# Counts for half blocks spread between the steps of two gates, and two ScalarE tables loaded ahead

## The chip, the cores and the metric

The kernel runs on one core of a Trainium2 chip. A core has five engines, each with an instruction stream of its own that runs in order: TensorE (PE; its weight loads are listed as PEld), VectorE (DVE), ScalarE (ACT), GpSimd (POOL) and SyncE (SP). [...] Transfers run on 16 DMA engines and are issued from the queues of SP, ACT and POOL; an issuing engine stands still while an issue waits. The metric is the device time of one execution in microseconds (us), as the median of several runs, lower being better.

## The reference

The input `x` has 8 × 256 rows of 512. Two layers follow one another, each added to its input:

```python
x = x + _L0_xattn_ref(_layernorm(x), k, fside_S2_0, ctx_2048, ctx_2048, 8)
x = x + _L0_ffn_ref(_layernorm(x), gate_w, shared_wg, ..., exp_wd)
```

The first layer is a long convolution by FFT of products of `v` with the context, per head (32 heads), summed with the context again. The second is a mixture of experts:

```python
scores = sigmoid(xf @ gate_w.T)
topk_w, topk_idx = top_k(scores, 2)
topk_w = topk_w / (topk_w.sum(-1) + 1e-20) * 2.5
shared_out = silu(xf @ shared_wg.T) * (xf @ shared_wu.T) @ shared_wd.T
h = silu(einsum('td,efd->etf', xf, exp_wg)) * einsum('td,efd->etf', xf, exp_wu)
routed_out = (topk_w[..., None] * einsum('etf,edf->etd', h, exp_wd)[topk_idx, t]).sum(1)
```

There are 2048 tokens, 8 experts of width 352 and a shared expert of width 704; each token goes to its two best experts.

## The kernel before

The 2048 rows are 16 tiles of 128 rows, and the tokens of the second layer are 4 chunks of 4 tiles. The order of all instructions is written out by hand (`tc.manual_schedule()`): an engine executes its instructions in the order in which the Python code emits them. Three stages follow one another.

**The loop over 32 heads** (lines 1481 to 1639) computes the convolution with products of Toeplitz matrices on TensorE (`conv_products`), weighs and sums on VectorE (`weigh`), and puts steps of the shared expert of the chunks that are ready between them. For a step that is a "seven" (seven products of half blocks in place of eight, `begin_seven`), `between` starts the first two products amid the head's convolution, and `copies`, called when the convolution is emitted, has ScalarE copy their results out of PSUM.

**The stage between** (lines 1642 to 1806) has no convolution left. It finishes the last tile's normalisation, the routing of the last chunk, the counts from which the blocks of tokens follow, and the table of tokens. The generator `rest_of_steps` supplies TensorE with the remaining steps of the shared expert, and `advance(n)` lets it run n pieces on, so the code alternates by hand between the two. Within it, a step's front products and their copies are emitted first, then `settle()` does what the steps before owe on VectorE and ScalarE, then come the step's other products. What a step owes is held in the list `owed`:

- for a down step, `rest` (line 1031): two adds of L1033 and two stores from SP's queue;
- for a seven of the up step, `gate` (line 912): it asks for a load of later weights, adds on VectorE (L914), and applies SiLU on ScalarE (L916). It returns `up`, whose add (L920) and multiply (L923) `settle` emits behind all gates.

The steps at issue are the last chunk's, c = 3, of which ft counts the tiles of the shared expert's width. In ft = 0 to 4, `product(1, p21, 3, ...)` writes the bank that the copies of `back` read, so it waits for a copy of L861 that stands behind a SiLU of L916 in ScalarE's order.

The counts: `route_places` (L793 to L804) gives each token its place and has POOL scatter the table's entries (L806); `block_experts` (L1147 to L1200) counts full blocks; `half_experts` (L1203 to L1294) counts half blocks, some 45 small VectorE instructions that mostly depend on one another. Its results are `eh` (the experts of half blocks), `any_half` (a matrix that picks the table's rows, read by TensorE in `half_slots`) and `used` (how many half blocks there are). They are emitted in one piece ahead of `advance(9 + 7 + 3)`, so all of them stand before the gates' adds of ft 0 and 1 in VectorE's order. `load_table` (L1299, SP) then brings the table, and `slots` and `half_slots` turn it into row numbers and gates with products L1326 to L1348.

ScalarE holds one set of function tables at a time. A load (ACT_TABLE_LOAD) is placed by the compiler ahead of a function whose set isn't there. The root (L329), SiLU (L916) and the sigmoid (L728 and, where c is 2, L977) are of different sets; copies and scaling by Identity need none of their own. The last tile's chain through ScalarE is: SiLU of the last seven of chunk 2, root of the variance (L329), normalisation (L354), a copy (L441), then four transposes on TensorE (L359).

**The block stage** (lines 1811 to 2021) goes through 33 blocks of up to 128 token rows: POOL gathers rows (L1732), SP stores and brings them back in squares (L1741, L1748), VectorE transposes (L1782, L1890), TensorE multiplies (up L1836, down L1906), ScalarE scales (L1915), and POOL adds the result into the output by a scatter (L1919). The shared expert's last two tiles are computed last and added to rows that are loaded when the scatters have ended (L2007 to L2021).

Of the kernel before, what the change touches and what calls it, by code (L numbers as in the profile page):

```python
# [8 lines left out]
F32 = mybir.dt.float32  # L9
I32 = mybir.dt.int32  # L10
# [5 lines left out]
P = 128  # L16
# [66 lines left out]
def tile_xattn_moe(  # L83
# [77 lines left out]
    ones = const.tile([P, P], F32, name="ones")  # L161
    G.memset(ones, 1.0)

    A.activation(const.tile([P, 1], F32, name="table_first"), ones[:, :1], AF.Sqrt)
    filler = rows.tile([P, 2 * P], F32, tag="xg", name="filler")
    G.memset(filler, 0.0)
    ident = kept.tile([P, P], F32, name="ident")
# [725 lines left out]
    def begin_seven(c, ft):  # L893

        n = c * NSF + ft
        w = ups.pop(n)
        if not isinstance(w, list):
            w = [w[:, b] for b in range(14)]
        if ft == 0:
            hTs[c] = held.tile([P, NSF, TC], F32, tag="hT", name=f"hT_{c}")  # L900
        pair = ps_acc.tile([P, 2, TC], F32, tag="acc", name=f"gu_{c}_{ft}")
        g = shp.tile([P, TC], F32, tag="g", name=f"g_{c}_{ft}", bufs=2)
        u = hTs[c][:, ft, :]

        def rhs(k, at):
            return xfT[c][:, k : k + 2].rearrange("p k i t -> p k (i t)")[:, :, at]

        first, second = slice(0, HT), slice(HT, TC)
        moving = rhs(0, first), rhs(2, first), rhs(2, second), tbs[c]
        front, front_copies, back, free_of, products, copied = seven(pair, w, moving, g, u)  # L910

        def gate():
            ask(n)
            ins = V.tensor_tensor(pair[:, 0], pair[:, 0], g, ALU.add)  # L914
            free_of(ins, products[1] + copied[1][-1:])
            silu = A.activation(g, pair[:, 0], AF.Silu)  # L916

            def up(parts=(0, 1)):
                if 0 in parts:
                    ins = V.tensor_tensor(pair[:, 1], pair[:, 1], u, ALU.add)  # L920
                    free_of(ins, [silu])
                if 1 in parts:
                    V.tensor_tensor(u, pair[:, 1], g, ALU.mult)  # L923

            return up

        return front, front_copies, back, gate
# [4 lines left out]
    def seven_step(c, ft):  # L932
        at = up_step, c, ft
        if at not in begun:
            begun[at] = begin_seven(c, ft)
            yield from begun[at][0]()
            begun[at][1]()
        _, _, back, gate = begun.pop(at)
        yield from back()
        owed.append(gate)  # L940

    asks, held_back = [], [False]

# [199 lines left out]
    def g(name, s, dtype=F32):  # L1143
        return const.tile(s, dtype, name=name)
# [58 lines left out]
    def half_experts(kinds, both_kinds, ends):  # L1203

        nblk, halves, fours = [kinds[:, n] for n in range(3)]
        most = NEXP - 1
        V.tensor_scalar(nblk, nblk, 2.0, None, ALU.mult)
        first = g("first", [P, NEXP])
        V.tensor_tensor(first, nblk, first_of, ALU.add)
        bounds = g("bounds", [P, 2 * NEXP])  # L1210
        V.tensor_scalar(bounds[:, :NEXP], ends[:, 0], 2.0, None, ALU.mult)
        begin = g("begin", [P, 1])
        V.tensor_scalar_max(begin, bounds[:, most:NEXP], 2.0 * NDYN)
        V.tensor_scalar(bounds[:, NEXP:], ends[:, 1], begin, None, ALU.add)
        skip_by = g("skip_by", [P, 2 * NEXP])
        V.tensor_scalar(skip_by[:, :NEXP], nblk, -1.0, float(HALVES), ALU.mult, ALU.add)
        V.tensor_tensor(skip_by[:, NEXP:-1], skip_by[:, :most], nblk[:, 1:], ALU.add)
        V.tensor_tensor(skip_by[:, NEXP:-1], skip_by[:, NEXP:-1], halves[:, :most], ALU.subtract)
        turn = skip_by[:, most:NEXP]
        V.tensor_scalar(turn, turn, nblk[:, 0:1], bounds[:, most:NEXP], ALU.add, ALU.add)  # L1220
        V.tensor_scalar(turn, turn, begin, -float(HALVES * NEXP), ALU.subtract, ALU.add)
        V.memset(skip_by[:, -1:], -1e5)
        n = NHALF // 2
        segs = [P, n, 2 * NEXP]
        scratch = small.tile([P, TC], F32, tag="lg", name="past_half")
        past = scratch[:, : n * 2 * NEXP].rearrange("p (i e) -> p i e", e=2 * NEXP)
        half = g("half", [P, NHALF])
        for at in (slice(0, n), slice(n, NHALF)):
            V.tensor_tensor(
                past,  # L1230
                halfno[:, at].unsqueeze(2).to_broadcast(segs),
                bounds.unsqueeze(1).to_broadcast(segs),
                ALU.is_ge,
            )
            V.tensor_tensor(past, past, skip_by.unsqueeze(1).to_broadcast(segs), ALU.mult)
            V.tensor_reduce(half[:, at], past, AX.X, ALU.add)
        V.tensor_tensor(half, half, halfno, ALU.add)


        which = g("which", [P, NEXP])  # L1240
        V.scalar_tensor_tensor(which, fours, float(FOURS), ends[:, 2], ALU.mult, ALU.add)
        V.tensor_tensor(first, first, both_kinds, ALU.add)
        V.scalar_tensor_tensor(first, first, float(FOURS), fours, ALU.add, ALU.mult)
        behind = g("behind", [P, 1])
        V.tensor_scalar_max(behind, bounds[:, 2 * NEXP - 1 :], float(SURE_ENDS))
        more_fours = fourno[:, NFOUR:]
        V.tensor_scalar(more_fours, more_fours, behind, None, ALU.subtract)
        V.scalar_tensor_tensor(
            more_fours, more_fours, float(FOURS + 1 + NFOUR), more_fours, ALU.is_ge, ALU.mult
        )  # L1250
        any_four = [P, NFOUR + NCOND, NEXP]
        found = scratch[:, : (NFOUR + NCOND) * NEXP].rearrange("p (i e) -> p i e", e=NEXP)
        V.tensor_tensor(
            found,
            fourno.unsqueeze(2).to_broadcast(any_four),
            which.unsqueeze(1).to_broadcast(any_four),
            ALU.is_equal,
        )
        V.tensor_tensor(found, found, first.unsqueeze(1).to_broadcast(any_four), ALU.mult)
        four = g("four", [P, NFOUR + NCOND])  # L1260
        V.tensor_reduce(four, found, AX.X, ALU.add)
        tail = half[:, NPAIR:]
        V.scalar_tensor_tensor(tail, four, -float(FOURS), tail, ALU.add, ALU.max)

        experts = [P, NHALF, NEXP - 1]
        past = scratch[:, : NHALF * (NEXP - 1)].rearrange("p (i e) -> p i e", e=NEXP - 1)
        V.tensor_tensor(
            past,
            half.unsqueeze(2).to_broadcast(experts),
            expert_thresh.unsqueeze(1).to_broadcast(experts),  # L1270
            ALU.is_ge,
        )
        of = g("of", [P, NHALF])
        V.tensor_reduce(of, past, AX.X, ALU.add)
        eh = kept.tile([P, NHALF], I32, name="eh")
        V.tensor_copy(eh, of)

        V.scalar_tensor_tensor(of, of, -float(HALVES), half, ALU.mult, ALU.add)
        V.tensor_scalar(
            of, of, float(HALVES - FIXED_ENDS), -float(HALVES), ALU.is_ge, ALU.mult  # L1280
        )
        V.scalar_tensor_tensor(half, of, float(FIXED_ENDS), half, ALU.add, ALU.add)
        V.tensor_scalar(own_block, own_block, lane, None, ALU.is_equal)
        any_half = g("any_half", [P, 2, NHALF])
        for n in range(2):
            V.tensor_scalar(any_half[:, n], half, float(-n), lane2, ALU.add, ALU.is_equal)

        used = kept.tile([P, 1], I32, name="used")
        spare_fours = g("spare_fours", [P, 1])
        V.tensor_scalar(  # L1290
            spare_fours, ends[:, 2, most:], -float(NFOUR), 0.0, ALU.add, ALU.max
        )
        V.tensor_tensor(used, spare_fours, behind, ALU.add)
        return eh, any_half, used  # L1294

    def load_table():

# [183 lines left out]
    for h in range(H):  # L1481
# [21 lines left out]
        if ready and is_begun(*steps[done][1:]):  # L1503

            def between(at=steps[done][1:]):
                begun[at] = (begin_seven if at[0] is up_step else begin_down)(*at[1:])
                for _ in begun[at][0]():
                    pass

            def copies(at=steps[done][1:]):  # L1510
                begun[at][1]()

        held_back[0] = not odd and t - 1 in SQUARES
# [181 lines left out]
    route_T(last_c)  # L1695
    route_scores(last_c, lambda: advance(1))
    route_pick(last_c)
    advance(7)
    route_ranks(last_c)
    route_places(last_c)  # L1700
    ek, pick, *kinds = block_experts()
    eh, any_half, used = half_experts(*kinds)
    advance(9 + 7 + 3)
    tab = load_table()
    advance(4 + 6)
    load_wgu(4)
    advance(4)
    slots(tab, pick)
# [406 lines left out]
```

## Time and profile before

| | |
|---|---|
| median of 3 runs | 731.85 us (731.7, 731.85, 733.65) |
| the profiled execution's own time | 732.95 us |
| its span in the trace | 731.2 us |
| granted TensorE clock, mean | 0.998 |
| TensorE busy | 719.9 us |
| VectorE, ScalarE, POOL busy | 536.6, 227.5, 406.7 us |
| mean DMA rate | 181 GB/s |

A row of a timeline reads: start, duration, engine, line, operation, output and inputs, shape, number; in brackets, the idle time of the engine before it and what ended that. Times count from the start of the span. `PE` rows are products, modelled to their end, so that rows in sequence overlap a little. A line such as L916 is the line in the kernel's source before the change; behind the change the numbers are higher by 1 to 21.

### The profile page before, as it was taken

The numbers are of one execution on the slowest core, as the hardware profiler recorded it, in microseconds if no ns is written. First come the engines' busy times: TensorE is split into PE (matmuls) and PEld (weight loads), VectorE is DVE, ScalarE is ACT, GpSimd is POOL, SyncE is SP. The second block draws the span as 40 slices with busy tenths as digits, with TensorE's granted clock in tenths as the row PEclk, the third lists the DMA queues.
The fourth block names the chain that finished last, engine by engine and source line by source line (L and its number), as shares of the span: only waits on it lengthen the run. The fifth ranks groups of instructions, "written<-read, shape, count | busy, mean of one in ns | idle before, by whom it ended". The sixth has DMA issues, their size and how long they took to land.

```text
span 731.2 us, 10342 instructions
## 1 busy us (share of the span) xinstructions
PE 719.9 (98%) x3189; PEld 386.7 (53%) x3189; DVE 536.6 (73%) x1212; ACT 227.5 (31%) x459; POOL 406.7 (56%) x436
## 2 busy tenths in 40 slices
PE   9999999999999999999999999999999999999996
PEld 4333336555555655555665478455544553455552
DVE  4788889878777987777987584296767676767750
ACT  2222245745426554426435122111111111111110
POOL 7899998489876388784380422114244444453221
PEclk9999999999999999999999999999999999999999
DMA  8658748555624565623436968699975667567424
GB/s 301 239 178 284 278 146 278 170 121 189 227 89 158 180 158 151 226 94 122 151 69 191 384 169 278 185 268 287 284 174 112 126 140 189 126 134 170 82 34 86
DMA packets 91566, 132.16 MB, mean 181 GB/s; under 512 B 10928, under 2 KB 54960, under 8 KB 91504
## 3 DMA queue, kind: packets, MB, share of 16 engines
q1 hardware_dynamic: 69936, 93.89, 40.7%
q0 software_dynamic: 8544, 17.34, 13.1%
q10 hardware_dynamic: 13024, 20.19, 8.0%
q8 instruction: 28, 0.46, 0.3%
q14 instruction: 34, 0.28, 0.1%
HBM read 93.86 MB, written 37.52 MB: 180 GB/s over the span
## 4 chain that ended last, share of the span: by engine, by line
PE 62%; DMA 20%; issue 7%; DVE 5%; POOL 2%; ACT 2%; SPq 1%; POOLq 0%; DVEq 0%; ACTq 0%
PE cv L514 23%; PE gu L849 15%; DMA out_dram<-ys,row 11%; PE up L1836 7%; DMA out_dram<-ys,second_row 4%; PE dn L849 3%; PE y L1906 3%; PE same L556 2%; PE dn L1006 2%; PE gu L971 2%; DMA xv_d<-xn 2%; PE dn L1084 1%; POOL picked L1732 1%; DMA xq_f<-xn_d 1%; ACT xn L354 1%
## 5 line engine op out<-in xcount | busy, mean ns | idle before, releaser
L514 PE MATMUL cv<-kv,tz 64*64 64x512 f32 (+1 forms) x976 | 184.5, 597 | 0.0
L1836 PE MATMUL up<-wgu_sb,xT 128*128 128x352 f32 (+5 forms) x784 | 162.3, 460 | 0.4 <-PEq L1947 0.4
L1890 DVE STREAM_TRANSPOSE hTb<-h 32x96 f32<-32x96 f32 (+1 forms) x512 | 133.8, 261 | 7.8
L465 POOL TENSOR_TENSOR kv<-vT,ctxT 128x512 f32<-128x512 f32 x127 | 131.7, 1070 | 11.2 <-DVE top L748 3.9
L1836 PEld LDWEIGHTS up<-wgu_sb,xT 128*128 128x128 f32 (+2 forms) x784 | 92.5, 155 | 74.5 <-issue 37.2
L514 PEld LDWEIGHTS cv<-kv,tz 64*64 64x64 f32 (+1 forms) x976 | 65.1, 145 | 109.4 <-issue 88.0
L1919 POOL DMA_INDIRECT out_dram<-ys,row x33 | 50.5, 1530 | 119.0 <-ACT ys L1915 62.8
L1906 PE MATMUL y<-wd_sb,hTb 128*128 128x512 f32 (+11 forms) x294 | 90.7, 594 | 0.0
L590 DVE TENSOR_TENSOR prod<-cv,ctxT 128x1024 f32<-128x1024 f32 x64 | 78.2, 1221 | 16.1 <-PE cv L514 14.3
L849 PE MATMUL gu<-tb,wst 128*128 128x256 f32 x320 | 78.6, 381 | 1.3 <-ACT g L861 1.1
L599 DVE TENSOR_REDUCE convT<-prod 128x128 f32<-128x1024 f32 x64 | 78.1, 1220 | 2.2
L1732 POOL DMA_INDIRECT picked<-xn_d,row x33 | 35.3, 1068 | 67.0 <-DMA picked_d<-picked 26.5
L849 PEld LDWEIGHTS gu<-tb,wst 128*128 128x128 f32 x320 | 60.3, 190 | 18.1 <-issue 7.9
L1915 ACT ACTIVATE ys<-y,gate 128x512 f32<-128x512 f32 x33 | 22.7, 687 | 142.5 <-PE y L1906 138.0
L849 PE MATMUL gu<-xfT,wst 128*128 128x256 f32 x240 | 60.1, 386 | 1.0 <-DVE cv L587 1.0
L645 POOL TENSOR_TENSOR skip<-ctxT,w 128x512 f32<-128x512 f32 x16 | 17.3, 1078 | 73.8 <-ACT w L637 43.6
L1906 PEld LDWEIGHTS y<-wd_sb,hTb 128*128 128x128 f32 (+5 forms) x294 | 34.8, 155 | 42.7 <-issue 37.8
L1858 DVE TENSOR_TENSOR h<-h,up 128x352 f32<-128x352 f32 x32 | 16.7, 520 | 54.4 <-PE up L1836 52.1
L849 PEld LDWEIGHTS gu<-xfT,wst 128*128 128x128 f32 x240 | 44.2, 190 | 19.4 <-issue 11.3
L514 PE MATMUL cv<-kv,td 128*128 128x512 f32 x88 | 45.2, 596 | 0.0
L806 POOL DMA_INDIRECT table<-entries,to x32 | 31.6, 988 | 18.9 <-DVE to L804 8.1
L1851 ACT ACTIVATE h<-up 128x352 f32<-128x352 f32 x33 | 15.3, 464 | 73.5 <-PE up L1836 73.5
(269 smaller groups left out, 830.7 us busy)
## 6 DMA issues: line engine op xcount, KB each, us to landing
wst<-wst_d SPq DMA_DIRECT2D x17, 896.0 KB, 7.3
tz<-in_toep_dram SPq DMA_DIRECT2D x32, 384.0 KB, 3.2
wgu_sb<-in_egu_dram ACTq DMA_DIRECT2D x3, 2816.0 KB, 15.4
picked_d<-picked SPq DMA_DIRECT2D x33, 256.0 KB, 2.2
xg<-picked_d SPq DMA_DIRECT2D x132, 64.0 KB, 3.2
ctxT<-in_cT_dram SPq DMA_DIRECT2D x16, 384.0 KB, 4.8
x<-in_xv_dram SPq DMA_DIRECT2D x16, 256.0 KB, 3.7
x<-in_x_dram SPq DMA_DIRECT2D x16, 256.0 KB, 6.0
```

What stands on the lines that cost most here:

```text
L465: engine.tensor_tensor(kvs[h][:, at], v[:, :, cols].unsqueeze(2).to_broadcast([P, B, NH, NH]), ctxT[t][:, at, :, cols].unsqueeze(3).to_bro ...
L514: return T.matmul(banks[lb][cols], lhsT=w, rhs=x, start=first, stop=all(left[lb][n] == 0 for n in here),)
L590: V.tensor_tensor(prod, ps.rearrange("p k b j i -> p (k b) j i"), ctxT[t][:, 2 + 2 * n : 4 + 2 * n, :, cols] .rearrange("p k b i -> p (k b ...
L599: V.tensor_reduce(convT[t][:, two, :, cols].rearrange("p k b j -> p (k b) j"), prod, AX.X, ALU.add)
L806: ins = G.indirect_dma_start(out=table, out_offset=bass.IndirectOffsetOnAxis(ap=to[:, i : i + 1], axis=0), in_=entry[:, i, n, :], in_offse ...
L849: ins = T.matmul(ps, lhsT=w[2 * a + k], rhs=x[:, k], start=start and k == 0, stop=k == 1, skip_group_check=True,)
L1732: G.indirect_dma_start(out=picked[:n], out_offset=None, in_=xn_d, in_offset=bass.IndirectOffsetOnAxis(ap=row[:n, b : b + 1], axis=0), boun ...
L1836: ins = T.matmul(ps[at, m, :FF], lhsT=xTs[k][:, j].rearrange("p c b -> p (c b)")[:, at], rhs=weights(wgu_sb, k, e, (m * NLB + j) * FF, FF) ...
L1890: V.transpose(hT[q * Q : (q + 1) * Q, :n, c], hk[c * Q : (c + 1) * Q, q * NF * Q : (q * NF + n) * Q].rearrange("p (t a) -> p t a", a=Q),)
L1906: T.matmul(ps[at], lhsT=hT[:fw, ft].rearrange("p c b -> p (c b)")[:, at], rhs=weights(wd_sb, k, e, ft * L, L)[:fw], start=(ft == 0), stop= ...
L1915: A.activation(y[:n], ps[:n], AF.Copy, scale=gate[:n, k : k + 1])
L1919: ins = G.indirect_dma_start(out=out, out_offset=bass.IndirectOffsetOnAxis(ap=index[: at.stop - at.start, col : col + 1], axis=0), in_=y[a ...
```

## The change

`half_experts` becomes a generator. It emits everything up to L1248 at once and hands out its three result tiles, which are now allocated there; the rest is cut in five pieces. A new function `count_on` lets it go on by one piece. `gate` calls it behind the SiLU, and `up` behind the add and behind the multiply, so the pieces fall between the instructions of the gates of ft 0 and ft 1 of the last chunk. The list `counts_left`, which is empty at all other times, says whether there is anything to hand out; what is left after `advance(4 + 6)` is emitted then.

Besides, ScalarE applies SiLU to one column of a constant tile in two places: in head 31, ahead of the front copies of the last seven of chunk 2, and after `route_pick` of the last chunk. The compiler then places the loads of SiLU's table there.

```diff
-    A.activation(const.tile([P, 1], F32, name="table_first"), ones[:, :1], AF.Sqrt)
+    table_first = const.tile([P, 2], F32, name="table_first")
+    A.activation(table_first[:, 0:1], ones[:, :1], AF.Sqrt)
...
             silu = A.activation(g, pair[:, 0], AF.Silu)
+            count_on()
 
             def up(parts=(0, 1)):
                 if 0 in parts:
                     ins = V.tensor_tensor(pair[:, 1], pair[:, 1], u, ALU.add)
                     free_of(ins, [silu])
+                    count_on()
                 if 1 in parts:
                     V.tensor_tensor(u, pair[:, 1], g, ALU.mult)
+                    count_on()
...
+    counts_left = []
+
+    def count_on():
+        for rest in counts_left:
+            next(rest, None)
...
+        eh = kept.tile([P, NHALF], I32, name="eh")
+        any_half = g("any_half", [P, 2, NHALF])
+        used = kept.tile([P, 1], I32, name="used")
+        yield eh, any_half, used
         any_four = [P, NFOUR + NCOND, NEXP]
...
         V.tensor_tensor(found, found, first.unsqueeze(1).to_broadcast(any_four), ALU.mult)
+        yield
         four = g("four", [P, NFOUR + NCOND])
...
         V.scalar_tensor_tensor(tail, four, -float(FOURS), tail, ALU.add, ALU.max)
+        yield
...
         V.tensor_reduce(of, past, AX.X, ALU.add)
-        eh = kept.tile([P, NHALF], I32, name="eh")
+        yield
         V.tensor_copy(eh, of)
...
         V.scalar_tensor_tensor(half, of, float(FIXED_ENDS), half, ALU.add, ALU.add)
+        yield
         V.tensor_scalar(own_block, own_block, lane, None, ALU.is_equal)
...
         V.tensor_tensor(used, spare_fours, behind, ALU.add)
-        return eh, any_half, used
+        yield
...
             def copies(at=steps[done][1:]):
+                if h == H - 1:
+                    A.activation(table_first[:, 1:2], ones[:, 1:2], AF.Silu)
                 begun[at][1]()
...
     route_pick(last_c)
+    A.activation(table_first[:, 1:2], ones[:, 1:2], AF.Silu)
     advance(7)
     route_ranks(last_c)
     route_places(last_c)
     ek, pick, *kinds = block_experts()
-    eh, any_half, used = half_experts(*kinds)
+    counts_left.append(half_experts(*kinds))
+    eh, any_half, used = next(counts_left[0])
     advance(9 + 7 + 3)
     tab = load_table()
     advance(4 + 6)
+    for _ in counts_left.pop():
+        pass
     load_wgu(4)
```

## The prediction

> **What bounds the kernel now.** The page comes first: TensorE (PE) works through nearly the whole span, so only what lets it stand still, or what follows its last product, can change the time.
>
> ```profile
> span 731.2 us, 10342 instructions
> PE 719.9 (98%) x3189; PEld 386.7 (53%) x3189; DVE 536.6 (73%) x1212; ACT 227.5 (31%) x459; POOL 406.7 (56%) x436
> ```
>
> 11.3 us of the span are without a product. The timeline of TensorE, read for the rows that carry an idle time, says where: 1.32 at the start, 0.63 near 110 us, 0.96 at 388.99 (behind a VectorE add, L587), 0.45 at 571.87 (a branch), the last 6.5 or so behind the last product, and two places in the stretch that the change touches. Here they are with the group ahead of each:
>
> ```profile
> 400.69 1.02 PE L971 MATMUL gu<-xfT,wst 128*128 128x512 f32 x2
> 402.43 0.66 PE L359 MATMUL ptf<-ident,xn_kqa 128*128 128x128 f32 x4 [0.71 <-ACT xn_kqa L441]
> ...
> 432.27 1.89 PE L849 MATMUL gu<-xfT,wst 128*128 128x256 f32 x8
> 434.85 1.99 PE L849 MATMUL gu<-tb,wst 128*128 128x256 f32 x8 [0.69 <-ACT g L861]
> ```
>
> Groups overlap by some 0.16 us, so a bracket understates a stop. By starts: 10 products of L1006 take 4.29 in the chain, 0.43 each, so the transposes could begin at 400.69 + 0.86 = 401.55, and began 0.88 late; 8 rows of L849 take 1.73 (430.54 to 432.27), so the second group could begin at 434.00, and began 0.85 late.
>
> What held ScalarE there, by its timeline:
>
> ```profile
> 385.59 0.59 ACT L562 COPY same<-same 128x512 f32<-128x512 f32 x1
> 390.12 0.37 ACT L861 COPY g<-gu 128x256 f32<-128x256 f32 x1 [3.95 <-PE gu L849]
> ...
> 396.99 1.28 ACT L916 ACT_TABLE_LOAD   x1 [0.45 <-DMA xq_f<-xn_d]
> 398.28 0.60 ACT L916 ACTIVATE g<-gu 128x512 f32<-128x512 f32 x1
> 398.89 1.28 ACT L329 ACT_TABLE_LOAD   x1
> 400.19 0.29 ACT L329 ACTIVATE rstd_last<-mv_last,eps 128x1 f32<-128x1 f32 x1
> 400.91 0.81 ACT L354 ACTIVATE xn<-x,nb_last,rstd_last 128x512 f32<-128x512 f32 x1 [0.43 <-DVE nb_last L350]
> ...
> 408.25 0.18 ACT L728 ACTIVATE plT<-logit 128x32 f32<-128x32 f32 x1
> 424.70 0.37 ACT L861 COPY g<-gu 128x256 f32<-128x256 f32 x1 [16.26 <-PE gu L849]
> ...
> 431.60 0.37 ACT L861 COPY hT<-gu 128x256 f32<-128x256 f32 x1 [0.49 <-PE gu L849]
> 431.99 1.28 ACT L916 ACT_TABLE_LOAD   x1
> 433.93 0.60 ACT L916 ACTIVATE g<-gu 128x512 f32<-128x512 f32 x1 [0.66 <-DVE gu L914]
> 434.43 0.37 ACT L861 COPY g<-gu 128x256 f32<-128x256 f32 x1
> ```
>
> The first stop ends a chain that runs through two table loads; the second ends one that waits for VectorE's add of the gate. VectorE's timeline shows why the add is late: the counts for half blocks stand ahead of it in VectorE's order.
>
> ```profile
> 427.64 0.19 DVE L1248 SCALAR_TENSOR_TENSOR fourno<-fourno 128x32 f32<-128x32 f32 x1
> 427.86 0.46 DVE L1253 TENSOR_TENSOR past_half<-fourno,which 128x288 f32<-128x288 f32 x1
> ...
> 432.01 1.28 DVE L1033 TENSOR_TENSOR x<-dn,x 128x512 f32<-128x512 f32 x2
> 433.21 0.69 DVE L914 TENSOR_TENSOR gu<-gu,g 128x512 f32<-128x512 f32 x1
> ```
>
> **Does the end follow TensorE?** After 434.85 it waits 0.45 in all. At the end, the chain goes from the last scatter (717.88, 4.84) to the load of the late rows (722.85, 3.37), their adds and stores; that last scatter was released by ScalarE's L1915, which follows TensorE's last down product. So what TensorE gains at 402 and 434 arrives at the end, unless a transfer becomes late.
>
> **The change, part by part.** In the built order, TensorE, POOL and SP have the same instructions in the same order. ScalarE loses two table loads and gets two, each with a one-column function behind it. VectorE has the same set, reordered only between L1248 and the second multiply of L923.
>
> *First draw (head 31, ahead of the two front copies).* It adds 1.28 for the load and about 0.20 for the function (the row of the first one-column function, L164, is 203 ns). ScalarE is free from 386.18 to 390.12, so 1.48 ends near 387.7: nothing. What it takes away is the load at 396.99. SiLU then runs 396.99 to 397.59 (its add, L914, ended at 396.54), the load for the root 397.60 to 398.88. The root now waits for its input instead: VectorE's L322 ends at 398.91 + 0.18 = 399.09, so root 399.11 to 399.40. Next late is VectorE itself: L923 holds it from 399.01 to 399.67, so the reciprocal L348 starts near 399.69 instead of 400.52. From there the old distances hold: 0.39 to the normalisation (400.91 − 400.52), 1.52 more to the transposes (402.43 − 400.91): 401.60, against a place free at 401.55. Gain 0.83; with VectorE's usual overlap of some 0.07 all 0.88. I take 0.85.
>
> In these rows a load takes 1.28 and the next function starts 0.01 behind it; what it costs is what a chain waits for it. [...]
>
> *The counts in five pieces.* L1253 to L1293 take 432.01 − 427.86 = 4.15 us of VectorE. The two residual adds L1033 and the gate's add move ahead of them. Times here are on the old clock; both engines come 0.85 earlier. The adds' product ended at 422.47 + 1.13 = 423.60, so they run from 427.86 for 1.20 (433.21 − 432.01), the gate's add 429.06 to 429.75 (its products were done by 426.22 + 1.89 = 428.11). SiLU is now held only by ScalarE's own order, behind the copy that ends at 431.97: with the table there, it runs 431.98 to 432.58. Distance from SiLU's start to TensorE's product was 434.85 − 433.93 = 0.92, so the product could run at 432.90; its place is 434.00. The whole 0.85 goes, with 1.1 to spare.
>
> *Second draw (after the pick).* ScalarE is free from 408.43 to 424.70; 1.48 lies in 16.26: nothing. Without it the load would stand at 431.99 to 433.27 and the product come at 433.28 + 0.92 = 434.20, so 0.20 of the 0.85 is the draw's and 0.65 the pieces'. Alone it would bring nothing, since the add came at 433.21.
>
> *What is behind the pieces.* The last piece (halves' matrix, L1286) now stands ahead of ft 1's last multiply, which ran at 439.51 after 1.53 of idle; the multiply ahead of it was held up 1.38 too. Walking the order with the old durations from 429.75: first piece 0.95, up add 0.69 (431.4), second 0.7, multiply behind SiLU (432.58) to 433.3, third 0.93, next gate's add 0.69 (434.9), fourth 0.85 (435.8), up add behind its copy (436.88 + 0.37 − 0.85 = 436.4) to 437.1, last piece 0.6: 437.7. TensorE reads it at 445.85 − 1.70 = 444.15. Cover: 6 us. The experts and the number of half blocks (L1276, L1293) are read in the block stage, past 470.
>
> *Queues.* SP's order is the same. It was blocked at L275 until 430.73; the stores of x 10 and 11, issued behind that, no longer wait for VectorE, so the last shared weights (433.79) and the table (434.82) go up to 0.5 earlier. POOL's scatters follow VectorE, 0.85 earlier.
>
> **Sum.** 0.85 + 0.85 = 1.70 us. From below: the brackets alone, 0.71 + 0.69 = 1.40. From above: 0.88 + 0.85, and the group after the second stop took 1.83 (434.85 to 436.68) for its 1.73: 1.83. Profiled execution: 732.95 with a span of 731.2, 1.75 around it; so 731.25 and a span of 729.5. It lies 1.1 above the median of three, 731.85 (731.7 to 733.65), so the median becomes **730.15**, −0.23%. About 0.3%, 2.2 us, is what a measurement of this kernel can tell from no change.
>
> **Rivals.**
> 1. *The table's rows come late (slower).* The products of L1326 move from 445.31 to 443.61 and need the table. In the view of the transfers SP's queue falls silent at 441.5, so there were 3.8 us of cover. But the load of two experts' weights (2816 KB, ScalarE's queue, issued 439.47) also comes 1.7 earlier and shares the engines with what SP has left from 438.8, about a microsecond behind the issue as before: 0.6 of the 0.86 MB of 438 to 440 and 0.29 behind, 0.81 MB. Where both queues worked (418 to 422) they had 0.89 and 0.61 MB in 4 us; at SP's 0.22 MB per us the 0.81 take 3.7: 442.5, no wait. If the weights went first (2.88 MB at the 0.35 MB per us that they had alone, 8 us), the table would land near 449: a wait of 5.3, less 1.7: 735.4. It decides from a landing at 445.3. Against it: the sharing at 418. Chance 0.07.
> 2. *One stop stays.* A chain that I have as ended is held by something else in the same wait, as ScalarE's wait at 396.99 that is put down to a DMA. Then 0.85: 731.0. Against it: the load starts 0.04 after the queue's issue at 396.53 + 0.42. Chance 0.10.
> 3. *More than the stops.* The chain behind the last product, 4.84 + 3.37 and the stores, meets other traffic and is shorter; scatters at the end took 4.58 to 5.03, and the median of all copies of a block landed in 2.2 where those near 450 took 3.8. A further us: 729.1. Nothing in the order speaks for it, but it needs little. Chance 0.13.
>
> **How the numbers follow.** Forecast 0.70. The three runs spread over 1.95 us, so a median can lie about 0.7 off; the forecast's own range is 729.4 to 730.9. Faster by over 0.3% means under 729.65, 0.5 below the forecast: I give that 0.35 of the 0.70, and 0.11 of rival 3's 0.13, 0.36 in all. Slower (over 734.05) needs rival 1 in full, 0.06, or two medians that both lie badly, 0.02. The rest, 0.56, is within. Range: rival 3 less part of the spread, 728.7; rival 2 plus it, 731.7; outside are most of rival 1 and the tails.
>
> **What would show it.** In the changed kernel's timeline of TensorE the idle of 0.71 and 0.69 should be gone or under 0.1; two table loads should stand in ScalarE's idle at about 386.2 and 407.6; SiLU should follow its copies at once; the gate's add should come some 4 us earlier; the first product of L1836 (its new line), at 470.34, should come at 468.6. Wrong would be: a wait on the table at the slots' products, a new idle past 468, or a tail that grows.

## The result, and the profile after

The changed kernel took 734.57 us (median of 10 runs, 733.74 to 736.16) against 732.42 for the kernel before, measured beside it (10 runs, 731.7 to 734.05). The ratio is 1.003 with a 95% interval of 1.0021 to 1.0038: 2.15 us slower where 1.70 us faster was forecast, and outside the range. The profiled execution took 733.94, with a span of 732.2, 1.0 more than the span before.

In the following lines, as in the rest, line numbers behind the change are higher by 1 to 21. The timeline of TensorE in the stretch of the change shows both places of the forecast:

```profile
396.38 2.74 PE L1016 MATMUL dn<-wshd,hT 128*128 128x512 f32 x6
400.67 1.12 PE L1016 MATMUL dn<-wshd,hT 128*128 128x512 f32 x2 [1.55 <-DVE hT L926]
401.63 1.02 PE L981 MATMUL gu<-xfT,wst 128*128 128x512 f32 x2
403.44 0.66 PE L360 MATMUL ptf<-ident,xn_kqa 128*128 128x128 f32 x4 [0.79 <-ACT xn_kqa L442]
...
427.24 1.89 PE L850 MATMUL gu<-xfT,wst 128*128 128x256 f32 x8
429.96 1.97 PE L850 MATMUL gu<-tb,wst 128*128 128x256 f32 x8 [0.84 <-ACT g L862]
...
432.63 1.89 PE L850 MATMUL gu<-tb,wst 128*128 128x256 f32 x8
434.35 1.89 PE L850 MATMUL gu<-xfT,wst 128*128 128x256 f32 x8
```

The second stop (0.69 at 434.85) is gone. The first (0.71 at 402.43) stands at 403.44 with 0.79, and ahead of it is a new one of 1.55, behind VectorE's multiply of the last seven of chunk 2. A stop of 0.84 at 429.96 is new too. All brackets between 386 and 450 sum to 0.23 + 1.55 + 0.79 + 0.84 = 3.41 us (the 0.23 stands at 390.66); in before they were 0.96 + 0.71 + 0.69 = 2.36. The difference, 1.05, is what the span grew by (1.0).

The timeline of ScalarE shows what the multiply waited for:

```profile
388.85 1.28 ACT L1527 ACT_TABLE_LOAD   x1
390.14 0.20 ACT L1527 ACTIVATE table_first<-ones 128x1 f32<-128x1 f32 x1
...
395.28 0.37 ACT L862 COPY hT<-gu 128x256 f32<-128x256 f32 x1 [2.45 <-PE gu L850]
395.94 3.31 ACTq L1683 DMA_DIRECT2D wgu_sb<-in_egu_dram  x1
399.29 0.60 ACT L917 ACTIVATE g<-gu 128x512 f32<-128x512 f32 x1 [3.64 <-issue]
399.91 1.28 ACT L330 ACT_TABLE_LOAD   x1
401.20 0.29 ACT L330 ACTIVATE rstd_last<-mv_last,eps 128x1 f32<-128x1 f32 x1
...
409.47 1.28 ACT L1715 ACT_TABLE_LOAD   x1
```

The table was there and SiLU needed no load. But the row ahead of SiLU, the issue of the first routed weights (`load_wgu(0)`, two experts, 2816 KB), took 3.31 us. In before it took 0.42:

```profile
396.53 0.42 ACTq L1666 DMA_DIRECT2D wgu_sb<-in_egu_dram  x1
```

SiLU ran at 399.29, a microsecond later than with its load in before (398.28), and its multiply, the root and the normalisation followed. `ACTq` marks a row of ScalarE's sequencer: it isn't counted as busy, but SiLU behind it starts only as it ends (399.29 against 399.25).

### The profile page after: what moved, and what is told of

Same layout as the page of the kernel before. It is cut to its first block, busy times and chain, and to the rows that moved or that the text cites. A ratio compares the mean times of both kernels' runs of the same rounds, so it can differ in the third digit from the quotient of the medians.

```text
span 732.2 us, 10342 instructions
## 1 busy us (share of the span) xinstructions
PE 719.6 (98%) x3189; PEld 386.0 (53%) x3189; DVE 536.1 (73%) x1212; ACT 227.9 (31%) x461; POOL 406.2 (55%) x436
```

## The experiments

Each time is the median against the kernel before on the same chip, which scattered more on some chips than on others (beside e1 to e4 24 of its 25 runs took 730.64 to 732.94, beside h1 to h4 15 of 29 took over 735.3); the ratio and its interval are what to go by.

**One part at a time.** e1 has the five pieces alone, e2 the first draw alone, e3 the second alone, e4 is the changed kernel again. The edit of e2 and e3 is one call each, beside the two-column `table_first`:

```diff
             def copies(at=steps[done][1:]):
+                if h == H - 1:
+                    A.activation(table_first[:, 1:2], ones[:, 1:2], AF.Silu)   # e2
...
     route_pick(last_c)
+    A.activation(table_first[:, 1:2], ones[:, 1:2], AF.Silu)   # e3
```

> The five pieces alone, both one-column functions of ScalarE left out. Theory 1 (the draws move ScalarE's issue of the first routed weights, load_wgu(0), onto a load of code, and it takes 3.31 us in place of 0.42): without the draws the issue takes about 0.42 again, the first stop at 402 stays as in before (0.71), the second one goes: 0.65 to 0.85 us under before. Theory 2 (the pieces cost the time, because semaphore updates of TensorE come late while POOL's scatters run and VectorE's adds stand among them, 426 to 430): still 1 to 2 us over before, with ScalarE's copy of the first half of a step near 429 waiting some 2 us. Theory 3 (both are chance of the one profiled execution, the loss has another cause): neither shows, and the time says which part carries the loss.

> Before with the first draw alone (head 31, ahead of the two front copies). Theory 1: the issue of load_wgu(0) takes some 3.3 us again, SiLU behind it starts near 399.3 in place of 396.9, TensorE waits 0.8 at 402 still and about 1 us is lost: 0 to 1.5 us over before. Theory 2: the draw gains its 0.85. Theory 3: the issue takes 0.42 and the stop of 0.71 at 402 is gone, 0.85 under before, or the loss shows elsewhere.

> Before with the second draw alone (after the last chunk's pick). It stands behind load_wgu(0) in ScalarE's order, so theories 1 and 2 both expect no change (within 0.3 us of before, the add at 433.2 stays last). If it alone costs 1 us or more, the second draw carries the loss and theories 1 and 2 both fall.

> The changed kernel itself once more. Theories 1 and 2: about 2.1 us over before; theory 1 an issue of load_wgu(0) of some 3.3 us in the trace again, theory 2 ScalarE's copy waiting 2 us or more near 429 again. Theory 3: the two are not there again, and the time still lies 1.5 to 2.8 over.

| | this, us | before, us | ratio (95%) | issue of `load_wgu(0)` |
|---|---|---|---|---|
| e1, pieces | 731.99 | 731.57 | 1.0023 (1.0002 to 1.0043) | 0.42 |
| e2, first draw | 735.86 | 731.57 | 1.0067 (1.0047 to 1.0087) | 4.54 |
| e3, second draw | 731.67 | 731.57 | 1.000 (0.9985 to 1.0016) | 0.42 |
| e4, all | 734.9 | 731.57 | 1.0059 (1.0036 to 1.0082) | 4.99 |

The first draw carries the loss, and it is worse than in the first profile. TensorE in e2:

```profile
395.89 2.74 PE L1007 MATMUL dn<-wshd,hT 128*128 128x512 f32 x6
401.42 2.08 PE L1007 MATMUL dn<-wshd,hT 128*128 128x512 f32 x2 [2.79 <-DVE hT L924]
403.29 1.55 PE L972 MATMUL gu<-xfT,wst 128*128 128x512 f32 x2
```

Behind the stop of 2.79 two products take 2.08, where two of the same shape took 1.02 in before (400.69, L971): TensorE ran at half its clock for some products (granted clock 0.66 from 400 to 405). In e4, behind a stop of 3.24, the granted clock was 0.70 from 405 to 410, and the products lost another 1.7 us. The pieces did what they should in e1's profile: no idle row at 434, the products from there on 0.64 us further ahead of before, and 731.46 for that execution. But four of its 11 runs took 735.35 to 736.83; none of these four has a profile, and the median gained nothing. Theory 2 falls: in after a copy of ScalarE waited 2.46 us up to 429.44 where it waits 0.49 in before; e1 and e4 wait there as before does.

**The place in ScalarE's code.** The trace also records the transfers of code, some of 8 KB and some of 16; it doesn't name the engine that they are for. Counting all of ScalarE's rows, issues and semaphore rows too, one of 8 KB comes near row 448 in all 20 profiles, from 0.6 us ahead of that row's start to 3.4 behind it, so I take it for ScalarE's. With the draw that row is the issue of `load_wgu(0)`; in before it is the SiLU behind it. In the four held issues, that of f1 below among them, the code came 1.6 to 3.4 us after the issue began, and the issue ended 1.0 to 1.3 us behind the code. So theory C: two more instructions ahead of the issue are enough. f1 is before with two one-column copies and no draw, f2 the changed kernel with eight such copies, f3 the first draw with eight; f4 moves the issue.

```diff
         t, odd = divmod(h, 2)
+        if h in (28, 29):        # f1;  23 <= h < 31 in f2 and f3
+            A.copy(table_first[:, 1:2], ones[:, 1:2])
...
-    load_wgu(0)                  # f4
...
     second_norm(last_t, rstd_of(mv, "_last"))
+    load_wgu(0)                  # f4
     load_wgu(2)
```

> Before with two one-column copies on ScalarE (0.2 us each, in heads 28 and 29, no function table) and no draw: ScalarE's instructions behind them only stand two places later. Theory C (a load of ScalarE's code, 8 KB, falls due at a fixed place in its instruction stream, and where that place is the issue of load_wgu(0), the issue is held until the code has come): the issue takes 3 to 5 us in place of 0.42 as with the draw, the SiLU behind it starts at 401 or later, and the time is 2 to 4.5 us over before, though no table has moved. Theory T (the issue is long because a function stands behind it where a table load stood): the issue takes 0.42 and the time is that of before within 0.5 us.

> The changed kernel with eight one-column copies on ScalarE in heads 23 to 30. Theory C: the place where the code falls due is now eight instructions ahead of the issue of load_wgu(0), so the issue takes about 0.42 again, the stop of 0.71 at 402 goes, and the time is what I had forecast for the change: 1.4 to 1.8 us under before. Theory T: the issue still takes 3 to 5 us and the time stays 2 to 3.3 over.

> Before with the first draw and the same eight copies. Theory C: the issue takes about 0.42, the time is 0.6 to 0.9 us under before, 5 us under the first draw without the copies. Theory T: 3 to 5 us of issue, and 4 us over before.

> The changed kernel with load_wgu(0) moved behind the last tile's normalisation, next to load_wgu(2). Theory C: SiLU, root and normalisation no longer stand behind the issue, and what is at the place where the code falls due is no issue, so nothing is held: 1.4 to 1.8 us under before, unless the first weights, some 6 us later, are missed at the first up product (needed at about 469, landed at 411.9 before: 57 us of cover). Theory T: the issue itself is again long, but behind the chain, so the time is the same as by theory C; this kernel tells only whether the whole loss lies in what stands behind that issue.

| | this, us | before, us | ratio (95%) | issue | stop at the slots |
|---|---|---|---|---|---|
| f1 | 737.52 | 732.94 | 1.0073 (1.004 to 1.0105) | 4.69 | 0.66 |
| f2 | 734.76 | 732.94 | 1.0026 (0.9995 to 1.0056) | 0.42 | 1.68 |
| f3 | 736.85 | 732.94 | 1.0029 (0.9993 to 1.0065) | 0.42 | 1.13 |
| f4 | 736.54 | 732.94 | 1.0044 (1.0011 to 1.0077) | 0.66, then 3.99 | 4.13 |

ScalarE's timeline in f1, where no table has moved:

```profile
395.44 4.69 ACTq L1669 DMA_DIRECT2D wgu_sb<-in_egu_dram  x1
400.16 1.28 ACT L917 ACT_TABLE_LOAD   x1 [5.01 <-DMA wst<-wst_d]
401.46 0.60 ACT L917 ACTIVATE g<-gu 128x512 f32<-128x512 f32 x1
```

Two copies of 0.2 us made the kernel 0.7% slower. So it isn't the table and isn't the function behind the issue (theory T), since here a table load follows as in before; it is where the issue stands in ScalarE's instructions. The same in f2, with eight copies:

```profile
396.77 0.42 ACTq L1685 DMA_DIRECT2D wgu_sb<-in_egu_dram  x1
397.24 0.60 ACT L917 ACTIVATE g<-gu 128x512 f32<-128x512 f32 x1 [0.46 <-DMA xq_f<-xn_d]
397.86 1.28 ACT L330 ACT_TABLE_LOAD   x1
399.37 0.30 ACT L330 ACTIVATE rstd_last<-mv_last,eps 128x1 f32<-128x1 f32 x1 [0.23 <-DVE mv_last L323]
```

This is the chain as I had forecast it: SiLU right behind the issue, the root held by VectorE. TensorE has no idle row at 402 nor at 434; against before its products shift by −0.88 at the first place and −0.85 at the second. (f3, the first draw with the copies, has the −0.88 too.) Then it loses it all. TensorE in f2, and the first row of the slots in before, which didn't wait:

```profile
445.31 0.54 PE L1326 MATMUL slots_ps<-pick,tab 128*128 128x25 f32 x4
```

```profile
441.94 1.89 PE L850 MATMUL gu<-tb,wst 128*128 128x256 f32 x8
445.51 0.65 PE L1341 MATMUL slots_ps<-pick,tab 128*128 128x25 f32 x4 [1.68 <-DMA tab<-table]
...
447.91 3.46 PE L850 MATMUL gu<-xfT,wst 128*128 128x256 f32 x8
451.15 2.14 PE L850 MATMUL gu<-tb,wst 128*128 128x256 f32 x8
```

And f2's windows (window, its length, PE busy with the number of products, granted clock, DMA share, GB/s):

```profile
445.00:448.00 3.00, 2.49 (x21) 1.00 1.06 371
448.00:452.00 4.00, 4.00 (x12) 0.57 0.93 322
452.00:456.00 4.00, 4.00 (x20) 1.00 0.37 139
```

The products of the slots wait 1.68 us for the table. It was issued at 436.96 (434.82 in before) and is there near 445.5, too late for a TensorE that now wants it at 443.8. Behind the stop eight products take 3.46 in place of 1.97. Where the forecast gave 1.7 us, this execution ended with TensorE's last product 2.0 us later than in before. f4 missed what was expected: with the two issues side by side the second took 3.99 and held ScalarE's copy of the last tile's transposed rows (TensorE idle 2.63 at 407.83), and the table came late by 4.13.

**Is it the table?** In the g runs `load_wgu(2)` is issued ahead of `load_wgu(4)`, some 38 us later, to take its 2816 KB out of the way of the table's scatters: g1 on top of f2, g2 on before alone, g3 on the pieces alone. g4 is f2 again.

```diff
     second_norm(last_t, rstd_of(mv, "_last"))
-    load_wgu(2)
...
+    load_wgu(2)
     load_wgu(4)
```

> The changed kernel with the eight copies, and load_wgu(2) issued behind the last pieces, right ahead of load_wgu(4), in place of behind the last tile's normalisation. Theory D (with the issue of load_wgu(0) short again, what eats the gain is the table: its scatters land late beside the 2.8 MB of load_wgu(2), so the products of the slots wait, and behind a stop of over a microsecond TensorE gets half its clock for some products): the scatters meet less traffic, the table is issued by 435 and there when TensorE reaches the slots at 443.7; no idle time there, clock 1.00, 1.4 to 1.8 us under before. Against it: the later weights may meet the gathers of the first blocks (449 to 455); then the gain shows up to 468 and is lost in a stop at the first up products. Theory E (the loss of the eight-copies kernel is scatter of that chip, not the table): no difference to the kernel with eight copies alone.

> Before with load_wgu(2) moved in the same way, and nothing else. Both theories: the table was in time in before, so within 0.5 us of before; it tells what the move does alone, above all whether it costs something past 449.

> The five pieces alone with load_wgu(2) moved. Theory D: the second stop goes and the table waits for nothing, 0.7 to 0.9 us under before, and no runs 4 us above the others as the pieces alone had (in 4 of 11). Theory E: such runs remain.

> The changed kernel with the eight copies once more. Theory D: the issue of load_wgu(0) takes 0.42 in this profile too, the slots' products wait 0.5 to 2 us for the table, and the time lies between 1.5 under and 2.5 over before, by what the table does in that run. Theory E: no wait there, 1.4 to 1.8 under before.

g1: 732.66 against 733.59, ratio 0.9992 (0.9972 to 1.0013). g2: 733.04, 0.9987 (0.9956 to 1.0017). g3: 732.86, 0.9994 (0.9974 to 1.0014). g4: 734.06, 1.000 (0.9976 to 1.0024). g4 repeats f2: issue 0.42, shifts of −0.88 and −0.85 at the two places, 1.61 of waiting for the table, half clock behind it:

```profile
445.44 0.65 PE L1341 MATMUL slots_ps<-pick,tab 128*128 128x25 f32 x4 [1.61 <-DMA tab<-table]
...
448.64 3.76 PE L850 MATMUL gu<-xfT,wst 128*128 128x256 f32 x8
```

No profile of g1 to g3 has a wait at the slots, but g1's profiled execution, 738.15, was its slowest: a stop of 3.25 at 391.98 had made TensorE late by then, so it doesn't test the table. None of g3's runs lies 4 us above the others (its slowest is 735.07), as theory D had it. In g2 the table was issued at 436.74, not earlier than 434.82, and SyncE still waited 1.7 us for the scatters: the move doesn't bring the table forward, and this profile speaks against the weights as its cause, which theory D took for granted.

**Ask for the table later.** h1 is f2 with eight pieces of products (in the trace 32 products of 256 columns, 6.9 us) moved from behind the slots to ahead of them. h2 is that move on before, h3 on the pieces alone. h4 is the first draw with ten copies, which puts row 448 on another issue, the store of a normalised tile. i1 is h1 again, i2 is h1 with `load_wgu(2)` moved too.

```diff
     load_wgu(4)
-    advance(4)
+    advance(4 + 8)
     slots(tab, pick)
...
-    advance(4 + 7 + NLB)
+    advance(4 + 7 + NLB - 8)
     block_T(seq[0])
```

> The changed kernel with the eight copies on ScalarE, and eight of the pieces of products that stood behind the slots now ahead of them (16 products of 0.43 us: TensorE asks for the table 6.9 us later). Theory D (the issue and the table are all that stood between the change and its forecast): the issue of load_wgu(0) takes 0.42, no idle time at 402 and 435, none at the slots (they come at about 450.5, the table landed at 445.5 in the two profiles with eight copies), clock 1.00 from 440 to 460, and 1.3 to 1.8 us under before. Against it: the rows of the blocks are gathered 5 us later than in before; the first block's transposition was done at 459.9 and its product ran at 470.3 in before, so some 10 us of cover less 1.7 and 5. If they are missed, TensorE stops at the first up products instead.

> Before with the slots moved behind eight more pieces, and nothing else. Theory D: the table was in time in before, so the time is that of before within 0.4 us; what it differs by is what the move does alone.

> The five pieces alone with the slots moved. Theory D: the second stop gone and no wait for the table: 0.6 to 0.9 us under before, without the runs at 735 to 737 that the pieces alone had in 4 of 11.

> Before with the first draw and ten copies in place of eight. By theory C, in its sharp form, ScalarE's row 448 is where code falls due (it was the issue of load_wgu(0) with the draw alone, a copy of L638 with eight copies, the SiLU in before); with ten copies it is the issue of the last store of normalised rows, L438: that issue is held in place of 0.33 for 1 us or more, the copy of L638 behind it starts that much later, and the issue of load_wgu(0) takes 0.42. If C in that form is wrong, both issues are short.

> The changed kernel with eight copies and the slots behind eight more pieces, once more, since its interval ended at 1.000. Theory D: 0.1 to 0.25% under before again (0.7 to 1.8 us), clock 1.00 behind 440, no idle time at 402, 435 and the slots.

> The same with load_wgu(2) issued ahead of load_wgu(4) as well. Theory D: the table is in time either way, so the same as without that move within 0.4 us; if the scatters that land sooner take away the delays of ScalarE's copies near 430 (0.8 to 1 us of idle time in several of these profiles), up to 1 us less.

| | this, us | before, us | ratio (95%) |
|---|---|---|---|
| h1 | 733.41 | 735.38 | 0.9981 (0.9962 to 1.0000) |
| h2, control | 734.28 | 735.38 | 0.9987 (0.9967 to 1.0008) |
| h3, pieces | 734.53 | 735.38 | 0.9992 (0.9968 to 1.0016) |
| i1, h1 again | 731.51 | 735.57 | 0.9958 (0.9936 to 0.9979) |
| i2, both moves | 731.82 | 735.57 | 0.9968 (0.9946 to 0.9990) |

With the issue short and the table asked for later, the kernel with the change is faster than before: 0.1% to 0.25% had been expected of i1, 0.42% was measured, with an interval from 0.21% to 0.64%. The forecast's 1.70 us (0.23%) lies inside it, and h1, the same kernel on another chip, came to 0.19% with an interval that reaches no change. TensorE in i1 at 391, at the place of the second stop, at that of the first wish for the table, and at the slots:

```profile
391.68 1.23 PE L850 MATMUL gu<-xfT,wst 128*128 128x256 f32 x4 [2.84 <-DMA wst<-wst_d]
...
435.72 1.89 PE L850 MATMUL gu<-xfT,wst 128*128 128x256 f32 x8
437.45 1.89 PE L850 MATMUL gu<-tb,wst 128*128 128x256 f32 x8
439.17 1.03 PE L850 MATMUL gu<-xfT,wst 128*128 128x256 f32 x4
...
455.05 0.54 PE L1341 MATMUL slots_ps<-pick,tab 128*128 128x25 f32 x4
```

No row carries a bracket at 402, at 435 or at the slots; behind 391.68, up to the branch at 574.71, TensorE has no stop. (The one at 391.68 came with 3.41 us at half clock, and this execution, 735.65, was the slowest of its 12; what it waited for is told in the last section.) From 400 to 441 its products gain 1.88 us on before's, in i2 and f2 as well, where 1.70 was forecast. The control alone isn't told apart from no change. The control h2 ran beside h1 only, and their intervals overlap, and no run has the eight copies alone; that the gain is the change's and not the move's rests on the rows: both stops gone, where h2 still shows 0.71 at 403.62 and falls 0.57 further behind before from 400 to 441. h3 tells nothing on the pieces' runs above 735: four of its 12 took over 735.3, but so did half of before's runs on that chip. The move of `load_wgu(2)` adds nothing (i2).

h4 (737.09, one run) goes against theory C in its sharp form. ScalarE:

```profile
393.21 0.33 ACTq L438 DMA_DIRECT2D xn_d<-xn  x1
...
397.64 0.45 ACTq L1673 DMA_DIRECT2D wgu_sb<-in_egu_dram  x1
```

The code came at 393.13 and took 2.00, so the place did move onto the store (row 448), and the issue of the weights was short. But the store's issue of 256 KB took its usual 0.33. So an issue at the place where code falls due isn't always held. On ScalarE all the held ones at that place were the 2816 KB. Size alone doesn't decide it, for SyncE has held issues of 256 and 896 KB (last section); what decides it stays open.

## Why the prediction was wrong

**First draw, −0.85 forecast: the step that failed.** It said that SiLU then runs from 396.99, right behind the queue's issue "at 396.53 + 0.42". I had taken the issue's 0.42 as a price of its own and moved it with everything else. In the changed kernel it is 3.31 and 4.99 in the two profiles, and the first stop, 0.71 in before, became 1.55 + 0.79 in the one and 3.24 with 1.7 of slow products in the other. By the starts of the products around it, that is 1.9 and 4.3 us more where 0.85 less was counted; f1 shows that two instructions more, without any table, are enough for it. With the place moved away (f2, g4) the term is −0.88 in both, close to what was worked out.

**The pieces and the second draw, −0.85 forecast: right in the rows.** In after, f2 and g4 the shift at 434.85 is −0.85; with the pieces alone (e1) −0.64, where 0.65 was given for them. The second draw alone does nothing (e3); the difference of 0.21 fits the 0.20 it was given. But part of this is luck of the execution: where TensorE also stops near 430 (below), the second stop is absent without the change too. From 425 to 441 g2 and h2, without the pieces, then fall 0.46 and 0.57 behind before, g3 and h3, with the pieces alone, 0.45 and 0.55, after and g4 0.12 and 0.07. No median of the pieces alone (e1, g3, h3) shows a gain clear of noise.

**Rival 1, the table, 0.07: right in its place, much too small in its chance.** It said that the table decides from a landing at 445.3, and I put the landing at 442.5 from the transfer rates. In f2 and g4 it landed near 445.5. Its working took the issue at 434.8 or earlier and 7.7 us from there to the landing. The issue came at 437.0 in f2 and 437.9 in g4, because SyncE's earlier issue of shared weights waited until 432.70 in f2 and 433.69 in g4 (430.73 in before), by the profile for a load of routed weights, and the table stands behind it. In after it came at 437.2, because the scatters landed late (SyncE waited 3.0 us for them). Where the trace shows the landing, it took 7.4 to 9.4 us (e1, f3, f4, i1) and 3.9 in i2, where `load_wgu(2)` is issued later. In after itself TensorE was so late by then that the table cost nothing.

**What no step had: the clock.** Every stop at the slots of 1.13 us or more (f2, f3, f4, g4, h4) was followed by products at half clock (granted clock 0.57 from 448 to 452 in f2, 0.50 from 455 to 460 in f4), and TensorE's last product came another 1.8 to 4.0 us later than the stop alone makes it. Rival 1 priced the wait alone.

**The stop of 0.84 at 429.96** isn't the change's: ScalarE's copy came 2 us behind its product there, and g2 and h2, which have no part of the change, show the same (0.87 and 0.98). The 0.96 at 388.99 in before comes and goes as well (last section). The forecast's chance for slower, 0.08, had room for the table and for badly lying medians only: that the change could make a row of unchanged work longer was not among the rivals.

## What to carry to other kernels

An instruction that is added for nothing still moves all that stand behind it on its engine (two one-column copies in f1, and the issue of `load_wgu(0)` took 4.69 us in place of 0.42): after such an edit, compare the durations of the issue rows behind it, and if one has grown, add or take a few instructions ahead of it before judging the idea. When a stretch is made faster, list for each input of the next stage when it landed and when it will be asked for, with several profiles if they can be had, and put more than a small chance on the one with the least cover. Price a stop at more than it lasts where the clock may follow it: the five at the slots of 1.13 to 4.13 us cost 1.8 to 4.0 us more, though no half clock followed the 1.55 at 400.67 in after.

## What the runs showed of the hardware

- **A held issue.** Four profiles of three kernels show the same issue at 3.31 to 4.99 us, the fifteen others that keep it in its place in the code show 0.42 to 0.45. Code that comes near row 448 does not always go with a late row: in before it came at 400.96 and took 0.31 with no row late, and in h4 at 393.13 with the store's issue at its usual 0.33; in e2, e4, f1 and the changed kernel it went with 2.9 to 4.6 us more of issue. Why the issue of 2816 KB is held there and the store of 256 KB in h4 isn't stays open.
- **Held issues on SyncE.** In 16 of the 20 profiles an issue of SyncE near 377 us took 2.42 to 4.50 us: in eleven that of 256 KB of x, which takes 0.43 in the others, in five (before, g1, h1, i1, i2) that of 896 KB of shared weights ahead of it, which takes 0.38 in the others. Each ended 0.13 us behind an 8 KB transfer of code that took 2.2 to 4.4 us; for which engine, the trace doesn't say.

```profile
377.10 3.29 SPq L294 DMA_DIRECT2D wst<-wst_d  x1
```

This row of before, and its like in the other four, set TensorE back: in those five profiles the product that reads these weights stands behind a stop, 0.96 us in before and 2.72 to 3.25 in the rest, and in no other. In before the weights landed at 388.85 and the product began at 388.99; the VectorE add that the bracket names ended at 388.88, but in the fifteen profiles without the stop that product begins ahead of the add. Such a hold can come and go between executions of one kernel: the changed kernel's first profile has the issue of x held (2.42 us), e4 neither.

- **Half clock after short stops.** The spells at half clock inside these kernels lasted 3.41 us (as in e2, f1 and f2), or two or three times that (6.83 in f3, 10.24 in f4). They followed stops of 1.13, 1.25, 1.61, 1.68 and 4.13 us at the slots, of 2.79 to 4.22 at 401 to 404 and of 2.84 and 3.25 near 392 (i1, g1). None followed the 1.55 at 400.67 in after, nor one of 2.63 at 407.83 in f4, of 2.72 at 391.43 in i2 or of 2.93 at 394.71 in h1; near 191 us one followed 2.01 in h1 and none 2.27 in h4. So 1.13 us was enough at the slots in f3, and 2.93 was not at 394.71 in h1; what decides it, no run shows.
- **Late reading.** In the changed kernel's first profile and in seven of the eighteen behind it a stop of 0.79 to 0.98 us stands near 430, in kernels with and without the change, while POOL's last scatters of the table are under way (issued from 417 to 427 in before). What delays ScalarE there was not tried.
